# Fewer, longer transfers at the end of a graph attention layer: x of blocks 24 to 27 in one load, results of 8 to 23 stored by four blocks, 28 and 29 in one store

## The chip, the cores and the metric

The kernel runs on one core of a Trainium2 chip. The metric is the device time of one execution in microseconds (us). The kernel before took 235.53 us, the median of three runs (235.43, 235.53 and 236.7).

A core has five engines that work side by side, each with its own order of instructions: TensorE (PE; PEld is its weight load), VectorE (DVE), ScalarE (ACT), GpSimd (POOL) and SyncE (SP, which here only issues DMAs). Engines wait for each other, and for DMAs, on semaphores. 16 DMA engines move the data between the chip's memory (HBM) and the on-chip buffers; they serve SP's queue of ordinary transfers (q1 in the profile) and GpSimd's queue of gathers (q0).

## The reference

`x` has 4096 rows of 512, `adj` is 4096 by 4096, `W` is 512 by 4 x 512, `a` holds 2 x 512 weights for each of 4 heads.

```python
ht = (h @ W).reshape(N, N_HEADS, N_HIDDEN).transpose(1, 0, 2)
src = jnp.einsum('hnd,hd->hn', ht, a_src)
dst = jnp.einsum('hnd,hd->hn', ht, a_dst)
e = jax.nn.leaky_relu(src[:, :, None] + dst[:, None, :], SLOPE) + adj_mat[None]
att = jax.nn.softmax(e, axis=-1)
h_prime = jnp.einsum('hij,hjd->hid', att, ht)
x = _layernorm(x + h_prime.mean(axis=0), axis=-1)
```

`adj` is added to the scores, and its entries reach 1e9. So in a row the column with the largest entry of `adj` takes the whole softmax, wherever it leads by more than the scores can differ.

## The kernel before

**What it computes.** `leading_rows` takes the leading column of each row: the output row is the layer norm of x[i] + x[column] times the mean of W over the heads. A bound on the scores, from the norms of x and of the heads' vectors, tests whether each row's leader leads by enough; only where a row fails does `general` (the full softmax) run, which it doesn't with these inputs.

**Blocks.** The 4096 rows are 32 blocks of 128, NB = 32; partition p holds rows 32p to 32p + 31, one of each block. So neighbouring blocks of one partition lie side by side in HBM: a transfer of n blocks of x or of the output moves n x 2 KB in one piece for each partition. `hold` has all 32 blocks of x, is overwritten by the results, and in its upper half (blocks 16 to 31) first holds W. Q is 4, LATE is 28, BEHIND is 24.

**One step of the loop** (line 423, t from 0 to 31): load adj of block t + 5 (2 MB; blocks 28 to 30 in two pieces, 31 in four); take the maxima over segments of adj's rows (DVE, line 169); find the leading segment and fetch it again by a gather on GpSimd (`find_segment`, `fetch_segment`: row L185, gather L191); for block t - 2 find the column in the fetched segment (`find_column`: L214, L216) and gather the rows of x (`gather_rows`, L202); for t - 3 turn these rows (PE, L229), copy them (ACT, L231) and multiply them by the mean of W (L244); for t - 4 the moments; for t - 6 the normalising.

**Blocks 24 to 27.** Their x is loaded late, at t = 31 (line 440), two blocks at a time, after adj of block 31 in SP's order. Their products are put by in a freed buffer of adj (`put_by`), and x is added after the loop: `add_x`, L261, for 24, 25 and 26 on GpSimd, for 27 on VectorE. ACT takes their row norms with `row_norm` (L251).

**After the loop** (lines 479 to 542) the order is written out by hand, and each engine keeps it. GpSimd's is: add x to 24 (line 486), column and gather of 30 (487), fetch of the segment of 31 (488), add x to 25 (489), gather of 31 (490), add x to 26 (491). The column of 31 is searched in the whole row of adj (L222). VectorE takes `find_inner` of blocks 24 to 31 (L208) and then the test (`bound(3)`, L392, and `test`), which needs the fetched segment of 31. TensorE's order is: turn of 30, last product of 29, count of the test (L409), three products of 30, turn of 31, last product of 30, products of 31 in two halves (L286).

**The stores.** SP issues the stores of blocks 0 to 7 by four, of 8 to 23 by two, and then, when each is ready, 28, 29, 24 with 25, 26 with 27, 30 and 31 (lines 482 to 485 and 540 to 542). SP waits, before each DMA that it issues, until the DMA eight before it in its order has landed: eight semaphores go round.

Of the kernel before, what the change touches and what calls it, by code (L numbers as in the profile page):

```python
# [68 lines left out]
def leading_rows(ctx, tc, x, adj, W, a, out, ident, v, n_bad, any_bad):  # L69
# [8 lines left out]
    nc = tc.nc  # L78
    N, D = x.shape
    H = a.shape[0]  # L80
    KB, NB, S = D // P, N // P, N // E
    S_EARLY = N // E_EARLY
    AHEAD = 5
    Q = 4
    PIECES = 4
    LATE = NB - Q
    BEHIND = LATE - Q
# [29 lines left out]
    def load_adj(ib):  # L117
        if 0 <= ib < NB:
            t = adj_t[ib] = adj_pool.tile([P, N], F32, name="adj_t")
            n = pieces(ib)  # L120
            for k in range(n):
                nc.sync.dma_start(t[:, ts(k, N // n)], adj_rows[ib][:, ts(k, N // n)])

    def load_x(lo, n):
        nc.sync.dma_start(hold[:, ds(lo, n), :], x_rows[:, ds(lo, n), :])
# [36 lines left out]
    def segment_maxima(ib, lo, hi):  # L162

        e = E_EARLY if ib < EARLY else E
        if lo == 0:
            seg_of[ib] = small.tile([P, N // e], F32, name=f"seg{e}", bufs=2)
        n = max(pieces(ib), 2)
        for k in range(lo * n // PIECES, hi * n // PIECES):
            nc.vector.tensor_reduce(  # L169
                seg_of[ib][:, ts(k, N // e // n)],  # L170
                adj_t[ib][:, ts(k, N // n)].rearrange("p (s e) -> p s e", e=e), axis=AX.X, op=OP.max,
            )

    def find_segment(ib):
        seg = seg_of.pop(ib)
        nc.vector.max(out=top[:, ib, :], in_=seg)
        at = at_of[ib] = small.tile([P, 8], U32, name="at")
        nc.vector.max_index(at, top[:, ib, :], seg)  # L178
        if ib < NB - 1:
            fetch_segment(ib)  # L180
# [29 lines left out]
    def find_column(ib):  # L210
        if ib < BEHIND:
            find_inner(ib)
        within = small.tile([P, 8], U32, name="within")
        nc.vector.max_index(within, top[:, ib, :], lead_of[ib])  # L214
        col = small.tile([P, 1], U32, name="col")
        nc.gpsimd.tensor_tensor(col, at_of.pop(ib), within[:, 0:1], op=OP.add)  # L216
        gather_rows(ib, col)
# [7 lines left out]
    def turn(ib):  # L225
        y = y_t.pop(ib)
        tp = psum.tile([P, KB, P], F32, name="tp", bufs=2)
        for kb in range(KB):
            nc.tensor.transpose(tp[:, kb, :], y[:, ts(kb, P)], ident)  # L229
        yt = yt_of[ib] = rows.tile([P, KB, P], F32, name="yt")  # L230
        nc.scalar.copy(yt, tp)  # L231

    def residual(ib):
        start = ib not in o_ps
        if start:
            o_ps[ib] = psum.tile([P, D], F32, name="o")
        nc.tensor.matmul(o_ps[ib], ident, hold[:, ib, :], start=start, stop=False)  # L237

    def products(ib, lo=0, hi=KB):
        start = ib not in o_ps  # L240
        if start:
            o_ps[ib] = psum.tile([P, D], F32, name="o")
        for kb in range(lo, hi):
            nc.tensor.matmul(  # L244
                o_ps[ib], yt_of[ib][:, kb, :], w_sum[:, kb, :],
                start=(start and kb == 0), stop=(kb == KB - 1),
            )

    def row_norm(ib):
        sq = rows.tile([P, D], F32, name="sq")  # L250
        nc.scalar.activation(sq, hold[:, ib, :], AF.Square, accum_out=xx[:, ib : ib + 1])  # L251

    def put_by(ib):

        if ib == BEHIND:
            o_ps["by"] = adj_pool.tile([P, N // D, D], F32, name="adj_t")
        nc.scalar.copy(o_ps["by"][:, ib - BEHIND, :], o_ps.pop(ib))
# [12 lines left out]
    def rstd(i):  # L270
        nc.gpsimd.tensor_scalar(sd[:, i], sd[:, i], 1.0 / D, EPS, op0=OP.mult, op1=OP.add)
        nc.gpsimd.tensor_tensor(sd[:, i], sd[:, i], power[:, : i.stop - i.start], op=OP.pow)  # L272
        nc.gpsimd.tensor_mul(nm[:, i], nm[:, i], sd[:, i])
# [54 lines left out]
    def store(queue, lo, n):  # L328
        queue.dma_start(out_rows[:, ds(lo, n), :], hold[:, ds(lo, n), :])

    def mean_of_heads(kb):
        o = psum.tile([P, D], F32, name="o")
        for h in range(H):
            nc.tensor.matmul(o, ident, hold[:, w_at + kb * H + h, :], start=(h == 0), stop=(h == H - 1))  # L334
        nc.scalar.activation(w_sum[:, kb, :], o, AF.Copy, scale=1.0 / H)  # L335
# [5 lines left out]
    def turn_a():  # L341
        tp = psum.tile([P, KB, P], F32, name="tp", bufs=2)
        for k in range(KB):
            nc.tensor.transpose(tp[:, k, : 2 * H], a_rows[:, ts(k, P)], ident[: 2 * H, : 2 * H])
        nc.scalar.copy(at_d, tp[:, :, : 2 * H])

    def turn_w(kb, h):
        tp = psum.tile([P, KB, P], F32, name="tp", bufs=2)
        for k in range(KB):
            nc.tensor.transpose(tp[:, k, :], hold[:, w_at + kb * H + h, ts(k, P)], ident)  # L350
        wt = rows.tile([P, KB, P], F32, name="wt")
        nc.scalar.copy(wt, tp)  # L352
        return wt

    def head_vector(kb, h, wt):

        for k in range(KB):
            nc.tensor.matmul(  # L358
                pv[:, kb, h : 2 * H : H], wt[:, k, :], at_d[:, k, h : 2 * H : H],
                start=(k == 0), stop=(k == KB - 1),  # L360
            )

    def head_norms():
        nc.vector.tensor_copy(v, pv)
        vv = once.tile([P, KB, 2 * H], F32, name="vv")
        nc.vector.tensor_mul(vv, v, v)
        pn = psum.tile([P, KB, 2 * H], F32, name="px", bufs=1)
        nc.tensor.matmul(pn, ones, vv, start=True, stop=True)
        n2 = once.tile([P, 2 * H], F32, name="n2")
        nc.vector.tensor_reduce(n2, pn.rearrange("p k c -> p c k"), axis=AX.X, op=OP.add)  # L370
        nc.scalar.activation(n2, n2, AF.Sqrt)
        both = once.tile([P, H], F32, name="both")
        nc.vector.tensor_add(both, n2[:, :H], n2[:, H:])
        nc.vector.tensor_reduce(vn, both, axis=AX.X, op=OP.max)
# [48 lines left out]
    for t in range(NB):  # L423
        if t == NB // 2:
            tc.mark_branch_hint_location("general", engines=HINTED)
        if t in x_at:
            load_x(*x_at[t])
        if t + AHEAD == NB - 1:
            load_x(LATE, Q)
        load_adj(t + AHEAD)  # L430
        middle = 1 if t == NB - 1 else 2
        segment_maxima(t, 0, middle)
        if t >= COLUMN:
            find_column(t - COLUMN)
        segment_maxima(t, middle, PIECES)
        pair = FINISH <= t < BEHIND + FINISH and t % 2 == 0
        if pair:
            rstd(slice(t - FINISH, t - FINISH + 2))
        if t == NB - 1:
            for ib in (BEHIND, BEHIND + 2):  # L440
                load_x(ib, 2)
        find_segment(t)
        if t < 2:
            mean_of_heads(t)
        elif t == 2:
            mean_of_heads(2)
            mean_of_heads(3)
        if t == 0:
            turn_a()
        turned = [(*vectors[0], turn_w(*vectors.pop(0))) for _ in range(vectors_at.get(t, 0))]  # L450
        if t == 16:
            head_norms()
        ib = t - PROJECT
        if t == NB - 1:
            for late in range(LATE, NB):
                row_norm(late)
        if t == NB - 2:
            residual(LATE)
            residual(LATE + 1)
        if ib >= 0:  # L460
            turn(ib)
            if ib > BEHIND:
                products(ib - 1, KB - 1, KB)
            if ib < BEHIND:
                residual(ib)
        for some in turned:
            head_vector(*some)
        if ib >= 0:
            products(ib, 0, KB if ib < BEHIND else KB - 1)
        if t >= BEHIND + STATS:  # L470
            put_by(t - STATS)
        elif t >= STATS:
            stats(t - STATS)
            row_norm(t - STATS)
        if pair:
            finish(t - FINISH)
            finish(t - FINISH + 1)
# [1 line left out]
    for ib in range(BEHIND, LATE):  # L479
        row_norm(ib)  # L480
    nc.scalar.activation(xx, xx, AF.Sqrt)
    for ib in range(0, 2 * Q, Q):
        store(nc.sync, ib, Q)
    for ib in range(2 * Q, BEHIND, 2):
        store(nc.sync, ib, 2)
    add_x(nc.gpsimd, BEHIND)
    find_column(NB - 2)
    fetch_segment(NB - 1)
# [48 lines left out]
    moments(NB - 1)  # L537
    factor(NB - 1, shift=True)
    finish_in_halves(NB - 1)
    for ib, n in ((NB - 4, 1), (NB - 3, 1), (BEHIND, 2), (BEHIND + 2, 2), (NB - 2, 1)):  # L540
        store(nc.sync, ib, n)
    store(nc.sync, NB - 1, 1)

# [152 lines left out]
```

## Time and profile before

| | |
|---|---|
| median of three runs | 235.53 us |
| the profiled execution | 235.65 us |
| its span in the profile | 234.1 us |
| busy: PE, DVE, ACT, POOL | 197.5, 191.6, 111.6, 100.3 us |
| moved by DMA | 97.06 MB, 415 GB/s in the mean |
| x of 24 and 25: issued, from issue to landing | 193.05, 15.5 us |
| x of 26 and 27: issued | 195.79 |
| store of 0 to 3 issued, store of 31 issued | 199.23, 229.70 |
| gather of x for block 31: issued, from issue to landing | 215.40, 7.1 us |

Times inside an execution are us from the start of the span. A row of an engine's order of time gives the start, the busy time, the engine, the line, the operation, out<-in with shapes, how many were merged, and in brackets the idle time before and what ended it. In the chain of waits each row is the start, the time and what the end was waiting for then; "issue" is time in which nothing that the profile shows was waited for. A DMA row gives the number of transfers, the size of each and the median time from issue to landing. The digits of a slice are tenths of it busy, 9 for 90% or more.

### The profile page before, as it was taken

To read this page: it belongs to the slowest core of one execution; us is meant where nothing else is said; L and a number is where in the kernel's file an instruction comes from. 1 tells how busy PE (TensorE), PEld (TensorE's weight loads), DVE (VectorE), ACT (ScalarE), POOL (GpSimd) and SP (SyncE) were. 2 spreads that over 40 slices of the span, in tenths; PEclk is the share of its full clock that TensorE was granted. 3 is DMA by queue.
4 is the path that set the end of the run, shared out by engine and by line. 5 is a ranking of instruction groups with operands and counts; after the bars stand their busy time and mean duration, and the time that the engine had idled before them with its cause. 6 is when DMAs were issued, how large, how long until landed. Compare 5 with 4: busy or idle time off the path is not lost.

```text
span 234.1 us, 2486 instructions
## 1 busy us (share of the span) xinstructions
PE 197.5 (84%) x683; PEld 101.6 (43%) x683; DVE 191.6 (82%) x300; ACT 111.6 (48%) x267; POOL 100.3 (43%) x212
## 2 busy tenths in 40 slices
PE   0198959999999699999999599859899967999980
PEld 0034525765656356555544144324333423344360
DVE  0566885589929999999789986999999999989871
ACT  2003012155665447475768264645564654187561
POOL 2022232415524464646443642646465464557400
PEclk9999778999999999999999979999999999999997
DMA  6999999999999999999999999999999999999994
GB/s 243 432 428 417 445 419 434 418 444 420 433 422 427 430 424 433 426 419 431 434 427 427 429 433 424 419 436 419 435 428 417 425 427 421 413 426 419 416 386 179
DMA packets 12977, 97.06 MB, mean 415 GB/s; under 512 B 2072, under 2 KB 2584, under 8 KB 7200
## 3 DMA queue, kind: packets, MB, share of 16 engines
q1 hardware_dynamic: 9360, 88.08, 89.0%
q0 software_dynamic: 3584, 8.77, 9.5%
q8 instruction: 6, 0.10, 0.2%
q14 instruction: 11, 0.09, 0.1%
q10 hardware_dynamic: 16, 0.02, 0.0%
HBM read 88.47 MB, written 8.39 MB: 414 GB/s over the span
## 4 chain that ended last, share of the span: by engine, by line
DMA 48%; POOL 19%; issue 17%; DVE 11%; PE 2%; ACT 0%; POOLq 0%; DVEq 0%; ACTq 0%; SPq 0%
DMA adj_t<-in_adj_dram 41%; DVE seg L169 8%; POOL y L202 6%; POOL lead L191 5%; DMA y<-in_x_dram,col 3%; DMA lead<-in_adj_dram,row 2%; POOL sd L272 2%; PE o L286 2%; DMA a_rows<-in_L_gnn_a_dram 1%; DVE col L222 1%; POOL row L185 1%; POOL start L198 1%; POOL col L216 1%; POOL lead_early L191 1%; DVE at L178 1%
## 5 line engine op out<-in xcount | busy, mean ns | idle before, releaser
L169 DVE TENSOR_REDUCE seg<-adj_t 128x128 f32<-128x2048 f32 (+2 forms) x66 | 145.4, 2207 | 29.0 <-DMA adj_t<-in_adj_dram 29.0
L244 PE MATMUL o<-w_sum,yt 128*128 128x512 f32 x248 | 116.0, 609 | 0.7 <-ACT yt L231 0.7
L244 PEld LDWEIGHTS o<-w_sum,yt 128*128 128x128 f32 x248 | 44.8, 193 | 53.9 <-issue 42.4
L231 ACT COPY yt<-tp 128x512 f32<-128x512 f32 x32 | 18.8, 587 | 45.8 <-PE tp L229 45.7
L202 POOL DMA_INDIRECT y<-in_x_dram,col x32 | 30.8, 961 | 16.5 <-POOL col L216 15.4
L334 PE MATMUL o<-hold,ident 128*128 128x512 f32 x32 | 20.9, 815 | 14.6 <-DMA hold<-in_L_gnn_W_dram 14.6
L229 PE MATMUL tp<-ident,y 128*128 128x128 f32 x128 | 19.7, 276 | 13.7 <-DMA y<-in_x_dram,col 13.7
L237 PE MATMUL o<-hold,ident 128*128 128x512 f32 x52 | 26.8, 600 | 0.0
L229 PEld LDWEIGHTS tp<-ident,y 128*128 128x128 f32 x128 | 14.4, 141 | 26.8 <-issue 25.5
L185 POOL TENSOR_TENSOR row<-at,first 128x1 uint32<-128x1 uint32 x32 | 6.0, 188 | 43.7 <-DVE at L178 43.3
L352 ACT COPY wt<-tp 128x512 f32<-128x512 f32 x16 | 9.2, 586 | 31.5 <-PE tp L350 31.5
L191 POOL DMA_INDIRECT lead_early<-in_adj_dram,row x18 | 18.1, 1008 | 8.9 <-POOL row L185 8.9
L216 POOL TENSOR_TENSOR col<-start,within 128x1 uint32<-128x1 uint32 x31 | 5.8, 188 | 36.0 <-DVE within L214 36.0
L251 ACT ACTIVATE sq<-hold 128x512 f32<-128x512 f32 x32 | 19.8, 619 | 0.0
L358 PEld LDWEIGHTS pv<-at_d,wt 128*128 128x128 f32 x128 | 16.3, 191 | 6.8 <-ACT wt L352 3.7
L334 PEld LDWEIGHTS o<-hold,ident 128*128 128x128 f32 x32 | 8.1, 265 | 25.1 <-issue 20.2
L335 ACT ACTIVATE w_sum<-o 128x512 f32<-128x512 f32 x4 | 2.4, 598 | 33.0 <-PE o L334 33.0
L277 ACT ACTIVATE hold<-o,nm,sd 128x512 f32<-128x512 f32 x24 | 17.2, 769 | 0.0
L191 POOL DMA_INDIRECT lead<-in_adj_dram,row x14 | 14.0, 1003 | 7.0 <-POOL row L185 7.0
L268 ACT ACTIVATE sq<-o,nm 128x512 f32<-128x512 f32 x24 | 16.5, 687 | 0.8
L358 PE MATMUL pv<-at_d,wt 128*128 128x2 f32 x128 | 15.3, 244 | 0.6 <-ACT wt L352 0.6
L266 ACT ACTIVATE sq<-o 128x512 f32<-128x512 f32 x24 | 14.6, 609 | 0.0
(91 smaller groups left out, 150.8 us busy)
## 6 DMA issues: line engine op xcount, KB each, us to landing
adj_t<-in_adj_dram SPq DMA_DIRECT2D x28, 2048.0 KB, 31.7
adj_t<-in_adj_dram SPq DMA_DIRECT2D x6, 1024.0 KB, 28.0
out_dram<-hold SPq DMA_DIRECT2D x10, 512.0 KB, 14.3
hold<-in_L_gnn_W_dram SPq DMA_DIRECT2D x4, 1024.0 KB, 18.8
hold<-in_x_dram SPq DMA_DIRECT2D x2, 2048.0 KB, 36.5
hold<-in_x_dram SPq DMA_DIRECT2D x3, 1024.0 KB, 27.8
adj_t<-in_adj_dram SPq DMA_DIRECT2D x4, 512.0 KB, 19.7
out_dram<-hold SPq DMA_DIRECT2D x2, 1024.0 KB, 13.8
```

Source lines behind the costliest of these rows:

```text
L169: nc.vector.tensor_reduce(seg_of[ib][:, ts(k, N // e // n)], adj_t[ib][:, ts(k, N // n)].rearrange("p (s e) -> p s e", e=e), axis=AX.X, op ...
L191: nc.gpsimd.indirect_dma_start(out=lead, out_offset=None, in_=adj_segs_early if early else adj_segs, in_offset=bass.IndirectOffsetOnAxis(a ...
L202: nc.gpsimd.indirect_dma_start(out=y, out_offset=None, in_=x, in_offset=bass.IndirectOffsetOnAxis(ap=col[:, :1], axis=0),)
L229: nc.tensor.transpose(tp[:, kb, :], y[:, ts(kb, P)], ident)
L231: nc.scalar.copy(yt, tp)
L237: nc.tensor.matmul(o_ps[ib], ident, hold[:, ib, :], start=start, stop=False)
L244: nc.tensor.matmul(o_ps[ib], yt_of[ib][:, kb, :], w_sum[:, kb, :], start=(start and kb == 0), stop=(kb == KB - 1),)
L251: nc.scalar.activation(sq, hold[:, ib, :], AF.Square, accum_out=xx[:, ib : ib + 1])
L268: nc.scalar.activation(sq, o, AF.Square, bias=nm[:, i], accum_out=sd[:, i])
L277: nc.scalar.activation(hold[:, ib, :], o_ps.pop(ib), AF.Identity, bias=nm[:, i], scale=sd[:, i])
L334: nc.tensor.matmul(o, ident, hold[:, w_at + kb * H + h, :], start=(h == 0), stop=(h == H - 1))
L358: nc.tensor.matmul(pv[:, kb, h : 2 * H : H], wt[:, k, :], at_d[:, k, h : 2 * H : H], start=(k == 0), stop=(k == KB - 1),)
```

## The change

The two loads of x of blocks 24 and 25 and of 26 and 27 become one load of four blocks. The stores of blocks 8 to 23 go by four blocks (four stores of 1 MB) and not by two (eight of 512 KB). The stores of 28 and of 29 become one. In this stretch SP issues 11 stores and one load of x where it issued 16 stores and two loads.

```diff
@@ -437,8 +437,7 @@
         if t == NB - 1:
-            for ib in (BEHIND, BEHIND + 2):
-                load_x(ib, 2)
+            load_x(BEHIND, Q)
         find_segment(t)
@@ -479,10 +478,8 @@
     nc.scalar.activation(xx, xx, AF.Sqrt)
-    for ib in range(0, 2 * Q, Q):
+    for ib in range(0, BEHIND, Q):
         store(nc.sync, ib, Q)
-    for ib in range(2 * Q, BEHIND, 2):
-        store(nc.sync, ib, 2)
     add_x(nc.gpsimd, BEHIND)
@@ -537,7 +534,7 @@
     finish_in_halves(NB - 1)
-    for ib, n in ((NB - 4, 1), (NB - 3, 1), (BEHIND, 2), (BEHIND + 2, 2), (NB - 2, 1)):
+    for ib, n in ((LATE, 2), (BEHIND, 2), (BEHIND + 2, 2), (NB - 2, 1)):
         store(nc.sync, ib, n)
     store(nc.sync, NB - 1, 1)
```

The bytes, the arithmetic and the order of the transfers in SP's queue stay as they were, but that 28's result now goes with 29's.

## The prediction

> **What bounds the kernel now.** I read the page's slices first, then the chain of waits of the last 34 us, GpSimd's and TensorE's order of time there, and last the DMA packet records.
>
> The slices (40 of 5.85 us) and the DMA issues of the page:
>
> ```profile
> DMA  6999999999999999999999999999999999999994
> GB/s 243 432 428 417 445 419 434 418 444 420 433 422 427 430 424 433 426 419 431 434 427 427 429 433 424 419 436 419 435 428 417 425 427 421 413 426 419 416 386 179
> ...
> out_dram<-hold SPq DMA_DIRECT2D x10, 512.0 KB, 14.3
> ...
> hold<-in_x_dram SPq DMA_DIRECT2D x2, 512.0 KB, 15.5
> ```
>
> The DMA engines are full in every slice but the first and the last. The rate shows no drop where transfers shrink: 413 to 426 GB/s in the slices of the half-megabyte stores, 417 to 445 in those of the 2 MB loads. So only the last few us can be gained or lost by order. The chain there:
>
> ```profile
> 210.14 3.29 DVE col L222 x2
> 213.42 0.02 issue
> 213.44 1.28 POOL adj_t L261
> ...
> 215.40 7.09 DMA y<-in_x_dram,col
> 222.49 0.14 issue
> 222.62 0.63 PE tp L229 x4
> ```
>
> It ends with the gather of block 31's rows of x; the rest, turn, products, moments and normalising, takes 7.2 us from there to the last store, issued at 229.7. GpSimd's own order of time:
>
> ```profile
> 208.75 1.27 POOL L261 TENSOR_TENSOR adj_t<-adj_t,hold 128x512 f32<-128x512 f32 x1 [1.86 <-ACT sq L251]
> 210.22 0.19 POOL L216 TENSOR_TENSOR col<-start,within 128x1 uint32<-128x1 uint32 x1 [0.20 <-DVE within L214]
> 211.01 0.97 POOL L202 DMA_INDIRECT y<-in_x_dram,col  x1 [0.60 <-POOL col L216]
> 212.00 0.20 POOL L185 TENSOR_TENSOR row<-at,first 128x1 uint32<-128x1 uint32 x1
> 212.46 0.96 POOL L191 DMA_INDIRECT lead<-in_adj_dram,row  x1 [0.27 <-POOL row L185]
> 213.44 1.28 POOL L261 TENSOR_TENSOR adj_t<-adj_t,hold 128x512 f32<-128x512 f32 x1
> 215.40 0.96 POOL L202 DMA_INDIRECT y<-in_x_dram,col  x1 [0.67 <-issue]
> ```
>
> The first row is the sum that adds x of block 24. The page names ACT as its releaser, but that ACT work was over 0.6 us before; x of 24 landed at 208.54 (issued 193.05, 15.5 us), 0.21 us before it starts. From there GpSimd has 0.2 us of air up to the gather of block 31. Its last add ends at 214.72, VectorE's column of 31 at 210.21 + 4.42 = 214.63: the two arms that release that gather end 0.1 us apart.
>
> **The skill beside the trace.** "DMA: Bandwidth & Descriptors" (the Trainium skill), section "Rules for kernel authors", asks for transfers of at least 1 MiB, which would favour the change. This trace bears on it with the rates above, and with its packets: 0.160 us for one of 4 KB, 0.310 us for one of 8 KB, 0.085 us for one of 2 KB. Doubling a packet saves about 0.01 us of it, not a fixed cost of a transfer, as eight transfers are in flight. The same page, "Queues, rings and completion order", says that an engine alternates between its queues packet by packet. This trace agrees: gathers of y (4 packets of 4 KB an engine) land in 7.6 to 7.7 us while SP's packets are of 16 KB, in 6.6 to 6.7 while they are of 8 KB, and in 6.2 (block 30) while they are of 4 KB. I go by these rows: a gather beside 8 KB packets is about 0.5 us later than beside 4 KB ones.
>
> **The change, part by part**, all against the profiled execution: 235.65 us, of which 234.1 are the span and 1.55 lie around it.
>
> *Less packet time.* Stores of 8 to 23: 1024 packets of 4 KB become 512 of 8 KB, 1024 x 0.1597 - 512 x 0.3095 = 5.1 us of engine time; x of 24 to 27: 1.3; 28 and 29: 256 of 2 KB become 128 of 4 KB, 1.2. Together 7.6 us over 16 engines, 0.47 us. That shortens the queue, not the chain.
>
> *x of 24 to 27 in one.* SP waits for the landing of the transfer eight before, so the one transfer is issued at 193.05, as the first half was. It lands when all of it is there. The second half lands now at about 209.85 (the store that reuses its semaphore is issued at 209.91); 0.08 us fewer of packets make it 209.77. The first add on GpSimd then starts at 209.98 instead of 208.75. **Queued behind it**: column and gather of 30, segment row of 31 and its fetch, the add of 25, the gather of 31. With 0.2 us of air they all move by 1.23 - 0.20 = 1.03 us; the gather of 31 goes out at about 216.4. ScalarE's squares of 24 to 27 (from 209.63) move by 0.3 us and have 1.2 us of air before the turned copy at 213.67: nothing.
>
> *Stores of 8 to 23 by four.* Four transfers fall away here and one at the load, so each store waits for an earlier landing and goes out sooner (the last of them at about 205.5 instead of 215.5). SP's queue is first in, first out and full for 14 us: the bytes move in the same order, nothing gained. Their results were normalised by 195.5, so no store waits for data. But the gathers of 30 and 31 and the fetch of 31 now run beside 8 KB packets. The fetch of 31 is also queued behind the gather of 30, whose packets span 1.9 us beside 8 KB packets and 1.3 beside 4 KB: it lands 1.03 + about 0.5 = 1.5 us late, at 219.2 or so instead of 217.7.
>
> *28 and 29 together.* Block 28 now waits for 29, normalised at 222.1: its store goes out some 6 us later, about 223.6 with the rest of the delay. The queue holds the stores up to 23 until about 225 (now: 28 to 30 and 24 to 27 are 4.6 us of packets that end near 230, so 23 ends near 225.4): no gap opens before it. After it the queue has gaps of up to about 1 us, as 24 to 27 become ready late; below I use them.
>
> **Two arms meet at the turn of 31** (now 222.62).
> Arm one, the gather: issue 216.4 and 6.65 us gives 223.05. The present one took 7.09 because one of 16 engines finished 0.7 us after the others (landings at 221.75 and 222.49), where an instruction fetch of 8 KB fell among its packets. If that comes again, 223.9.
> Arm two, TensorE's order:
>
> ```profile
> 217.85 0.14 DVE L392 TENSOR_TENSOR lead_by<-px,vn 128x1 f32<-128x1 f32 x1
> ...
> 219.20 0.22 PE L409 MATMUL px<-gap,ones 128*1 128x32 f32 x2 [0.18 <-DVE gap L405]
> 219.35 2.84 PE L244 MATMUL o<-w_sum,yt 128*128 128x512 f32 x6
> 222.62 0.63 PE L229 MATMUL tp<-ident,y 128*128 128x128 f32 x4 [0.43 <-DMA y<-in_x_dram,col]
> ```
>
> The test needs the fetch of 31 (landed 217.71, so L392 follows at 217.85). The count and the products of 30 stand before the turn of 31, with 0.43 us of air. 1.5 us late, they end at 222.19 + 1.5 = 223.7.
> The later arm puts the turn at 223.3 to 224.1; I take 1.25 us late. The rest of the chain keeps its length: the last store is issued at 229.70 + 1.25 = 230.95.
>
> **The cover.** From the issue of the last store (now 229.70) to its first packet on a free engine is 0.84 us, its eight packets 0.7: done at 231.24 on fifteen engines. One engine still sends 4 KB packets of an earlier store until 230.9 and ends at 232.2; its completion is the one the end waits for. It lags since a 16 KB instruction fetch took it for 0.97 us at 225.9. After the change, the gaps between the late stores let such an engine catch up, so the last store ends on all engines at 230.95 + 1.55 = 232.5. The end moves by 232.5 - 232.2 = **0.3 us**: 235.65 + 0.3 = 235.95. The profiled execution stands 0.12 above the median, 235.53, so I write **235.9**.
>
> **Rivals.**
> 1. *The cover is gone* (slower). An instruction fetch or the longer backlog of 24 to 27 leaves one engine a full us behind at the end again, and the stray engine in the gather of 31 comes again as well: 1.25 to 1.5 us are paid in full, **237.0**. For it: fetches of 8 and 16 KB fall in this stretch now, and the delay moves them along with the work. Against it: the gaps of up to 1 us. It decides once the last store is issued later than about 231.8, or an engine's backlog passes that time.
> 2. *The queue is the bound* (not slower). If the add of x is not on the path, because x lands with its first half's time or GpSimd has more air than I read, only the 0.47 us of packets count: **235.1**. For it: the DMA is full to 229. Against it: most engines run empty between 230.3 and 230.5, before the last store's first packet.
> 3. *The transfers merge nothing on the chip*, as each is cut into rows of a partition anyway. Packets of 8 KB appear already where stores go by four, so this is not so.
>
> **Numbers.** My forecast 0.58, rival 1 0.27, rival 2 0.12, the rest something else. 0.5% or 1.2 us is what can be told from no change: 234.35 to 236.7. Rival 1 lies mostly above it, and a tenth of the forecast's spread too: slower 0.31. Rival 2 lies inside it for the most part: faster 0.06. Same 0.63. Range: down to rival 2, 235.0; up to rival 1 and a little more, 237.2.
>
> **What would show it.** The add of 24 starts near 210.0; the gather of 31 is issued near 216.4 and takes 6.6 to 7.6 us; L392 follows the fetch of 31 at about 219.3; the turn of 31 starts at 223.3 to 224.1; stores of 8 to 23 are all issued by 206; the last store is issued near 231.0 and lands within 2.3 us (now 3.1). I am wrong if the gather of 31 goes out where it did, or if the end follows some engine's backlog rather than the last store's own latency.

## The result, and the profile after

The changed kernel takes 236.1 us in the median of 15 runs (235.89 to 238.03), the kernel before 235.56 (15 runs, 235.38 to 236.7). The ratio is 1.0034, with a 95% interval of 1.002 to 1.0048: 0.5 us slower in the median, 0.8 by the ratio. The profiled execution took 235.96 us with a span of 234.3; before it was 235.65 and 234.1. The executions of most kernels fall into a cheaper and a dearer group, whose shares differ between kernels (of the changed one eight lie at 235.89 to 236.10 and seven at 236.49 to 238.03), so below the lowest time stands beside each median.

The slices and the DMA issues of the changed kernel's page:

```profile
DMA  6999999999999999999999999999999999999984
GB/s 234 437 425 420 445 418 434 417 438 424 436 423 426 429 427 429 427 427 422 434 429 435 422 430 427 417 439 417 435 425 418 427 425 422 415 424 428 422 348 191
...
out_dram<-hold SPq DMA_DIRECT2D x6, 1024.0 KB, 19.2
...
out_dram<-hold SPq DMA_DIRECT2D x3, 512.0 KB, 4.3
```

The rate while the stores run (slices 34 to 38: 422 to 428 but for one of 415) is hardly higher than before. The slice before the last fell from 386 to 348 GB/s: the same bytes are spread further towards the end. The 1 MB stores take longer from issue to landing because they are issued sooner and stand in the queue. What came late shows in GpSimd's order of time:

```profile
209.96 1.28 POOL L261 TENSOR_TENSOR adj_t<-adj_t,hold 128x512 f32<-128x512 f32 x1 [3.45 <-ACT yt L231]
211.19 0.19 POOL L216 TENSOR_TENSOR col<-start,within 128x1 uint32<-128x1 uint32 x1
211.66 0.97 POOL L202 DMA_INDIRECT y<-in_x_dram,col  x1 [0.27 <-POOL col L216]
212.64 0.20 POOL L185 TENSOR_TENSOR row<-at,first 128x1 uint32<-128x1 uint32 x1
213.11 0.96 POOL L191 DMA_INDIRECT lead<-in_adj_dram,row  x1 [0.27 <-POOL row L185]
214.09 1.28 POOL L261 TENSOR_TENSOR adj_t<-adj_t,hold 128x512 f32<-128x512 f32 x1
215.53 0.96 POOL L202 DMA_INDIRECT y<-in_x_dram,col  x1 [0.16 <-PE px L385]
```

The add of 24 starts at 209.96, 1.21 us later than before; the one load landed at 209.75. The gather of 30 and the fetch of 31 go out 0.65 us late, the gather of 31 only 0.13. The chain of waits now runs through the fetch of 31, no longer through the gather of 31:

```profile
213.11 6.30 DMA lead<-in_adj_dram,row
...
219.63 0.07 DVE lead_by L392
...
220.90 0.22 PE px L409 x2
221.12 2.77 PE o L244 x6
223.89 0.44 PE tp L229 x4
```

The fetch takes 6.30 us (before 5.25) and lands at 219.41, 1.70 late. The test, the count and the products of 30 follow it without a pause, and the turn of 31 starts at 223.73 where it started at 222.62.

### The profile page after: what moved, and what is told of

Its sections match the earlier page's. It is cut to its first block, busy times and chain, and to the rows that moved or that the text cites. A ratio compares the mean times of both kernels' runs of the same rounds, so it can differ in the third digit from the quotient of the medians.

```text
span 234.3 us, 2472 instructions
## 1 busy us (share of the span) xinstructions
PE 199.2 (85%) x683; PEld 103.2 (44%) x683; DVE 191.7 (82%) x300; ACT 111.6 (48%) x267; POOL 100.1 (43%) x212
## 4 chain that ended last, share of the span: by engine, by line
PE 28%; DMA 23%; issue 21%; POOL 21%; ACT 3%; DVE 2%; POOLq 0%; DVEq 0%
PE o L244 14%; DMA hold<-in_L_gnn_W_dram 11%; POOL y L202 6%; POOL lead L191 5%; DMA lead<-in_adj_dram,row 5%; DMA y<-in_x_dram,col 4%; PE pv L358 4%; DMA adj_t<-in_adj_dram 3%; PE o L237 3%; PE o L334 3%; POOL sd L272 2%; PE tp L229 2%; POOL lead_early L191 2%; PE tp L350 2%; PE o L286 2%
## 5 line engine op out<-in xcount | busy, mean ns | idle before, releaser
L334 PE MATMUL o<-hold,ident 128*128 128x512 f32 x32 | 21.9, 850 | 15.0 <-DMA hold<-in_L_gnn_W_dram 15.0
L237 PE MATMUL o<-hold,ident 128*128 128x512 f32 x52 | 27.7, 619 | 0.3 <-DMA hold<-in_x_dram 0.3
L229 PEld LDWEIGHTS tp<-ident,y 128*128 128x128 f32 x128 | 15.0, 143 | 24.8 <-issue 23.9
```

## The experiments

Three theories to begin with: *A*, the late load and the longer stores each delay the last gathers, and only together do they pass the air in TensorE's order and the cover at the end; *B* and *C*, the late load or the longer stores alone are the whole cost. The table has, from each profile, the times of the drain's chain. "F30" is when the fetch of 30's segment goes out, which measures how late the loop itself was; "F30 to turn" is from there to the turn of 31, so it compares drains alone. The landings are those of the DMA records. `reorder_b` and `kept_b` are the kernels `reorder` and `kept` profiled a second time: two profiles of one kernel differ by 0.22 and 0.46 us in "F30 to turn".

| kernel | F30 | gather of 30: issued, takes | fetch of 31 lands | F30 to turn of 31 | last store: issued, takes | median, lowest us |
|---|---|---|---|---|---|---|
| before | 204.23 | 211.01, 6.16 | 217.71 | 18.39 | 229.70, 3.14 | 235.56, 235.38 |
| the change | 203.97 | 211.66, 7.25 | 219.41 | 19.76 | 230.78, 2.39 | 236.1, 235.89 |
| x_one | 203.93 | 211.61, 6.65 | 218.82 | 19.21 | 230.19, 2.48 | 235.78, 235.4 |
| stores4 | 203.88 | 210.72, 6.98 | 218.19 | 18.81 | 229.77, 2.73 | 236.32, 235.05 |
| pair | 203.95 | 210.94, 6.28 | 217.66 | 18.58 | 229.61, 3.10 | 235.85, 235.44 |
| x_and_stores | 204.13 | 211.64, 7.28 | 219.42 | 19.61 | 230.79, 2.25 | 236.12, 235.65 |
| reorder | 205.06 | 211.79, 7.14 | 219.61 | 19.14 | 231.28, 2.41 | 236.0, 235.21 |
| reorder_b | 205.73 | 212.71, 7.33 | 220.51 | 19.36 | 232.17, 2.23 | 237.07, one execution |
| delay2 | 204.12 | 212.31, 6.25 | 218.99 | 19.19 | 230.36, 2.36 | 235.6, 235.29 |
| stores8 | 203.90 | 210.72, 8.62 | 221.20 | 21.61 | 232.56, 2.31 | 237.59, 236.91 |
| stores1 | 205.77 | 212.43, 6.08 | 219.03 | 18.00 | 230.82, 2.27 | 235.99, 235.71 |
| kept | 204.98 | 211.76, 6.52 | 218.95 | 19.14 | 231.20, 2.26 | 235.28, 234.98 |
| kept_b | 204.45 | 211.07, 6.59 | 218.35 | 18.68 | 230.21, 2.55 | 235.23, 235.06 |

**One part of the change at a time.** `x_one` has the load of four blocks alone, `stores4` the stores of 8 to 23 by four alone, `pair` 28 with 29 alone, `x_and_stores` the first two:

```diff
# x_one, x_and_stores
-            for ib in (BEHIND, BEHIND + 2):
-                load_x(ib, 2)
+            load_x(BEHIND, Q)
# stores4, x_and_stores
-    for ib in range(0, 2 * Q, Q):
+    for ib in range(0, BEHIND, Q):
         store(nc.sync, ib, Q)
-    for ib in range(2 * Q, BEHIND, 2):
-        store(nc.sync, ib, 2)
# pair
-    for ib, n in ((NB - 4, 1), (NB - 3, 1), (BEHIND, 2), ...
+    for ib, n in ((LATE, 2), (BEHIND, 2), ...
```

> Only x of 24 to 27 in one load. Theory A (two arms with 0.43 us of air, and an end covered by about 1 us by the slowest DMA engine; only load and stores together pass it): the add of 24 starts at 210.0, the gather of 30 goes out 0.65 us late (near 211.7), the fetch of 31 lands at 218.4 instead of 217.7, the turn of 31 starts near 222.9, and the end moves by -0.1 to +0.1 us. Rival B (the late x is the whole cost of the change): 0.4 to 0.6 us slower. Rival C (the stores are the whole cost): the fetch of 31 lands where it did.

Measured: ratio 1.0015 (1.0002 to 1.0027). The add of 24 starts at 209.91, the gather of 30 at 211.61. The fetch of 31 lands at 218.82, the turn of 31 starts at 223.14, a little later than theory A had it. C falls: the fetch moved although the stores are as before. The gather of 30 takes 0.49 us longer than in the kernel before, although 4 KB packets run beside it in both; theory A has no term for that. B isn't excluded by the time, whose interval, 0.05 to 0.6 us, holds B's range too; it falls with the next run.

> Only the stores of 8 to 23 by four. Theory A: GpSimd's order keeps its times; the gather of 30 takes 7.0 to 7.3 us instead of 6.2, the fetch of 31 6.0 to 6.3 instead of 5.2, so it lands near 218.7; the turn of 31 starts 0.5 to 0.7 us late, near 223.2, which the cover hides; 0.3 us fewer of packets: the time changes by -0.3 to +0.1 us. Rival B (the late x is the whole cost): 0.3 us faster, and the fetch of 31 lands where it did. Rival C (the stores are the whole cost): 0.4 to 0.6 us slower.

Measured: ratio 1.0016 (0.9997 to 1.0035), medians far apart, the lowest 0.3 us below. GpSimd's order keeps its pace, but the gather of 30 takes 6.98 us and the fetch of 31 6.01: it lands 0.48 late though the loop was 0.35 early. So B falls: the stores alone delay the fetch too. The time is unclear: six executions lie at 235.05 to 235.28, below the lowest of the kernel before (235.37), the other eight at 236.08 to 237.17. The profile is of one of the six, with a span of 233.5 against 234.1. Its turn of 31 comes 0.42 us later after F30, yet its last store lands 28.6 us after F30 as before: that delay is hidden. How much of the shorter span is the loop's early start, and how much the packets, the profile does not separate.

> Only 28 and 29 in one store. Theory A: the chain is untouched, the turn of 31 at 222.6; the store of 28 with 29 goes out at 222.1; 0.08 us fewer of packets: within 0.1 us of no change. Rival D (the late store of 28 leaves the queue empty and makes its end late): 0.3 to 0.7 us slower, with a gap in the DMA before 222 to 224.

Measured: ratio 1.0006 (0.9991 to 1.0021). The turn of 31 starts at 222.53, the last store at 229.61; the store of 28 with 29 goes out at 222.08. The DMA engines are full from 222 to 224 us (share 1.02, before 1.03), so the gap that D needs is not there; the time alone, -0.2 to 0.5 us, would not exclude D.

> The load in one and the stores by four, 28 and 29 apart. Theory A: the two delays add up on the fetch of 31, which lands 1.6 to 1.8 us late (near 219.4), the turn of 31 starts near 223.7, past the cover: 0.3 to 0.6 us slower, as the whole change. Rival D: no slower than before.

Measured: ratio 1.002 (1.0009 to 1.003), the fetch of 31 lands at 219.42, the turn of 31 starts at 223.74. These are the times of the whole change to 0.01 us, though its loop was 0.16 us later. In "F30 to turn" the load adds 0.82 us, the stores 0.42, both 1.22, the whole change 1.37: within the spread of two profiles the two add up. At the landing of the fetch, counted from F30, they add 1.41, 0.83 and together 1.81, less than the sum. The times of the runs are too close to split the 0.8 us the same way.

**Why the late load costs.** If it costs only because GpSimd's column, gathers and fetch are queued behind its add, moving that add behind them must give the time back. `reorder` is the whole change with

```diff
-    add_x(nc.gpsimd, BEHIND)
     find_column(NB - 2)
     fetch_segment(NB - 1)
-    add_x(nc.gpsimd, BEHIND + 1)
+    add_x(nc.gpsimd, BEHIND)
     find_column_in_row(NB - 1)
+    add_x(nc.gpsimd, BEHIND + 1)
     add_x(nc.gpsimd, BEHIND + 2)
...
-    stats(BEHIND + 1)
...
     turn(NB - 2)
+    stats(BEHIND + 1)
     stats(BEHIND + 2)
```

> The whole change, with GpSimd's add of x to 24 moved behind the fetch of 31's segment, the add to 25 behind the gather of 31, and ScalarE's sums of 25 behind the copy of 30. Theory A (the late x costs only because column, gathers and fetch are queued behind its add): gather of 30 near 210.9, fetch of 31 issued near 212.3 and landing near 218.3, turn of 31 near 222.7, last store near 229.8, and with 0.47 us fewer of packets a span of 233.3 to 233.7, 0.4 to 0.8 us below before. Rival B2 (the cost of the change lies in the packets beside the gathers alone): as the changed kernel, 234.1 to 234.4.

Measured: ratio 1.0021 (1.0004 to 1.0038); the lowest is 235.21. The span, 234.8, is not what A expected, but this execution came 0.83 us late into the drain. GpSimd's order of time in it:

```profile
211.00 0.19 POOL L216 TENSOR_TENSOR col<-start,within 128x1 uint32<-128x1 uint32 x1 [3.31 <-DVE within L214]
211.79 0.96 POOL L202 DMA_INDIRECT y<-in_x_dram,col  x1 [0.60 <-POOL col L216]
212.77 0.20 POOL L185 TENSOR_TENSOR row<-at,first 128x1 uint32<-128x1 uint32 x1
213.23 0.96 POOL L191 DMA_INDIRECT lead<-in_adj_dram,row  x1 [0.27 <-POOL row L185]
214.21 1.28 POOL L261 TENSOR_TENSOR adj_t<-adj_t,hold 128x512 f32<-128x512 f32 x1
```

The column waits for VectorE again, as before the change, and each row lies 0.77 to 0.78 us behind that of before, as the loop does (0.83): the late load no longer holds up GpSimd's order. F30 to turn is 19.14, 0.62 shorter than with the change. What is left, 0.75 us, comes with longer gathers: 7.14 us for that of 30, and 7.89 (before 7.09) for that of 31, which lands at 224.06, just ahead of the turn. So B2 is wrong on the mechanism: ten of the 22 executions, 235.21 to 235.43, lie below every one of the changed kernel. The median shows no gain over the kernel before.

> The reordered kernel once more, for a second profile: in the first the loop's work was already 0.8 us late when the fetch of 30 went out (205.06 instead of 204.23), by a longer stretch at half the clock near 82 us. With the fetch of 30 near 204 again, theory A expects the gather of 30 near 210.9, the fetch of 31 landing near 218.3, the turn of 31 near 222.9 and a span of 233.4 to 233.9.

Measured: one execution, 237.07 us, span 235.5. It didn't settle the span, as the loop was later still: the fetch of 30 went out at 205.73. F30 to turn is 19.36.

**Packets beside a gather.** `stores8` and `stores1` store 8 to 23 by eight blocks and by one:

```diff
-    for ib in range(2 * Q, BEHIND, 2):
-        store(nc.sync, ib, 2)
+    for ib in range(2 * Q, BEHIND, 2 * Q):   # stores8
+        store(nc.sync, ib, 2 * Q)
+    for ib in range(2 * Q, BEHIND):          # stores1
+        store(nc.sync, ib, 1)
```

> Stores of 8 to 23 by eight blocks, packets of 16 KB beside the last gathers; the rest as before. Theory A (a gather of y waits for one packet of SP's queue at each of its four): gather of 30 takes 8.0 to 8.6 us (before 6.2), fetch of 31 about 7.2 (before 5.2), the turn of 31 starts 1.0 to 1.8 us late: 0 to 0.8 us slower. Rival F (the longer gathers come from more stores standing in the queue, not from their packets): as with stores by four, 7.0 and 6.0 us.

> Stores of 8 to 23 one block at a time, packets of 2 KB; the rest as before. Theory A: gather of 30 takes 5.7 to 5.9 us, the chain is up to 0.3 us earlier, but the queue has 0.6 us more of packets and its slowest engine sets the end: 0.4 to 0.8 us slower. Rival E (the end follows the chain): 0 to 0.3 us faster.

Measured: `stores8` 1.0099 (1.0066 to 1.0132), `stores1` 1.0013 (1.0005 to 1.0021). The gather of 30 takes 6.08 us beside packets of 2 KB, 6.16 to 6.28 beside 4 KB, 6.98 beside 8 KB and 8.62 beside 16 KB where x of 24 to 27 comes in two loads. Where it comes in one, it takes 6.52 to 6.65 beside 4 KB and 7.14 to 7.33 beside 8 KB. In `stores4` and `stores8` all stores up to 23 stand in SP's queue when the gather goes out, the same bytes in six stores and in four, and the gather differs by 1.64 us: F falls. `stores8` cost more than expected, 2.0 us, because the fetch of 31 took 9.0 us, not 7.2. It stands behind the gather of 30 in GpSimd's queue, which was 2.5 us longer, and one DMA engine ended it at 221.20, the fifteen others by 220.38. `stores1` has the shortest chain of all (18.00), and is not faster. That speaks against E, but weakly: its profiled loop was 1.5 us late.

**The cover.** To delay the chain with no transfer changed, `delay2` and `delay4` put two and four idle adds on GpSimd:

```diff
     add_x(nc.gpsimd, BEHIND)
+    for k in range(2):                       # 4 in delay4
+        nc.gpsimd.tensor_add(o_ps["by"][:, Q + k, :], hold[:, 0, :], hold[:, 0, :])
```

> The kernel before, with two idle adds of 1.27 us each on GpSimd behind the add to 24; no transfer is changed. Theory A: gather of 30 and fetch of 31 go out about 1.9 us late, the turn of 31 starts 1.2 to 1.6 us late, and of that 0.7 to 1.0 us are hidden by the slowest DMA engine: 0.3 to 0.8 us slower. Rival E (nothing is hidden, the end follows the last store's issue): 1.2 to 1.6 us slower.

Measured: ratio 1.0003 (0.9989 to 1.0018). Its chain of waits:

```profile
213.76 5.23 DMA lead<-in_adj_dram,row
...
223.47 0.44 PE tp L229 x4
...
229.77 0.56 ACT hold L326
```

The turn of 31 is 0.69 us late, less than expected, the last store 0.66 late (230.36), and the span 234.0 against 234.1: all of it is hidden. The table says where: the last store takes 2.36 us instead of 3.14. In the kernel before, fifteen engines end that store by 231.86 and the last at 232.84; in `delay2` by 232.57 and at 232.72. In every kernel whose last store goes out after 230 this time is 2.2 to 2.55 us; where it goes out before, it is 2.7 to 3.1. The difference between 3.14 and 2.36, 0.8 us, is the cover. E falls.

> The kernel before, with four idle adds on GpSimd in place of two; no transfer is changed. With two, the turn of 31 started 0.7 us late and the end did not move. Two more are 2.55 us: the turn of 31 starts about 3.2 us late (near 225.8). Theory A (a cover of about 0.8 us at the end): the end moves by 2.2 to 2.6 us. Rival E (nothing is covered, the first 0.7 us were lost in the measurement): 3.0 to 3.3 us. Rival G (the queue can hide a delay of this size too): under 1.5 us.

Measured: ratio 1.0112 (1.008 to 1.0144), median 3.0 us slower, lowest 237.56, 2.1 above. G falls. The rest is unclear: the profiled execution (span 239.0) lost more at TensorE, whose clock was halved in the drain, so A and E can't be told apart here.

**What can be kept.** `kept` is `reorder` with the stores of 8 to 15, which stand beside the gather of 30 and the fetch of 31, by two again; `kept_b` is the same kernel once more.

```diff
-    for ib in range(0, BEHIND, Q):
+    for ib in range(0, 2 * Q, Q):
+        store(nc.sync, ib, Q)
+    for ib in range(2 * Q, 4 * Q, 2):
+        store(nc.sync, ib, 2)
+    for ib in range(4 * Q, BEHIND, Q):
         store(nc.sync, ib, Q)
```

> What the theory would keep of the change: x in one with the reordered adds, 28 and 29 together, stores of 16 to 23 by four, but 8 to 15, which are in flight beside the last gathers, by two. Theory A: gather of 30 about 6.2 us, fetch of 31 about 5.3 us as before, turn of 31 near 222.6, and 0.31 us fewer of packets: 0.1 to 0.4 us faster than before. Rival B2: no faster, or slower, as the x in one still costs.

> The kernel of the run kept once more, since its interval still holds no change: theory A expects 0.2 to 0.4 us faster in the median again, and a profile in which the fetch of 30 goes out near 204.2 as before, with gathers of about 6.2 us and a last store near 229.7.

Measured: `kept` 235.28 against 235.63, ratio 0.9992 (0.9975 to 1.0008); `kept_b` 235.23 against 235.6, ratio 0.9984 (0.9972 to 0.9997). The median is 0.35 us lower both times, and the second interval leaves no change just out. It is the best version tried, by about 0.15%. In the two profiles the gather of 30 takes 6.52 and 6.59 us and the fetch of 31 5.75 and 5.83, longer than I expected (6.2 and 5.3): beside 4 KB packets that is what `x_one` has too (6.65 and 5.75), so moving GpSimd's add does not take this part of the load's cost away. The gather of 31 still runs beside 8 KB packets (7.84 and 7.53 us, before 7.09), and the turn waits for it.

## Why the prediction was right

The forecast was 235.9 us; it is 236.1. The sum was made for the profiled execution, 235.95, which took 235.96; for the seven dearer executions it has no term. The mechanism is the one forecast: a late add and longer gathers delay the turn of 31, and the cover takes most of that. But two terms were off in opposite ways, 0.4 us too much and 0.6 too little, and that they nearly cancel is luck.

- *The add of 24 and what is queued behind it.* Predicted at 209.98, it starts at 209.96. "They all move by 1.03 us" was the mis-sized term: 0.65 for the gather of 30 and the fetch, 0.13 for the gather of 31. I took the pauses ahead of a gather for fixed. They fall from 0.60 to 0.27 and from 0.67 to 0.16 us when what the gather waits for has come before GpSimd gets there.
- *Gathers beside 8 KB packets.* "About 0.5 us later" was mis-sized the other way: 1.1 for the gather of 30 and 1.05 for the fetch. `stores4` shows 0.82 and 0.76 without the late load. The kernel before had that row: its gather of 29, issued at 205.93 beside stores with 8 KB packets, took 6.94 us; the 6.6 to 6.7 are gathers beside loads. The rest comes with the load in one, which lengthens the gather of 30 beside 4 KB packets as well (by 0.49 in `x_one`). Part of it passes before the gather's first packet: 4.17 to 4.35 us where x comes in two loads, 4.34 to 4.59 where it comes in one. Why stays open.
- *Two arms at the turn of 31.* The fetch was to land 1.5 us late and landed 1.70 late. TensorE's arm was to end at 223.7: its products end at 223.89, later by the fetch's 1.70, but the turn starts at 223.73 already, as the two overlap by 0.16 in the profile. The gather's arm was ready at 223.09 (223.05 predicted), by luck: it went out 0.9 us earlier than predicted and took 0.9 longer. The last store was to go out at 230.95 and went out at 230.78.
- *The cover.* The last store was to land within 2.3 us and took 2.39. Its landing moved by 0.33 us (232.84 to 233.17; 0.3 predicted), the span by 0.2. But its cause was wrong in one point. I put the slowest engine's lag down to the instruction fetch of 16 KB at 225.9. The landings show it earlier: the store of 12 and 13 ends on fifteen engines by 219.48 and on the last at 219.80, that of 14 and 15 by 221.34 and at 222.68. Between them falls the fetch of 8 KB at 220.2; that it is the cause was not tested. And the gaps did not let it catch up at once: in the changed kernel one engine still ends the store of 26 and 27 at 231.93, the others by 231.01. By the last store it has caught up (233.17, the others by 233.04).

The gaps themselves are there. The DMA share by stretches, before (the last two columns are the share and GB/s):

```profile
225.00:229.00 4.00, 2.64 (x13) 1.98 (x11) 2.92 (x12) 2.36 (x6) 0.00 (x0) 1.00 0.93 369
229.00:230.00 1.00, 0.00 (x0) 0.00 (x0) 0.53 (x2) 0.56 (x1) 0.00 (x0) 1.00 0.95 377
230.00:231.00 1.00, 0.00 (x0) 0.00 (x0) 0.00 (x0) 0.00 (x0) 0.00 (x0) 1.00 0.65 252
```

and in the changed kernel:

```profile
225.00:229.00 4.00, 3.72 (x17) 2.96 (x16) 3.28 (x11) 3.15 (x6) 0.00 (x0) 1.00 0.68 275
229.00:230.00 1.00, 0.00 (x0) 0.00 (x0) 0.57 (x4) 0.29 (x1) 0.00 (x0) 1.00 1.04 426
230.00:231.00 1.00, 0.00 (x0) 0.00 (x0) 0.61 (x2) 0.56 (x1) 0.00 (x0) 0.99 0.93 363
```

From 225 to 229 the engines now stand idle a third of the time, as 24 to 29 become ready late: the 0.47 us of packets that the change saves come back as idle time before the last results exist.

- *Rival 1* (237.0) has the time of the executions of 236.5 to 237.1, but no profile of the changed kernel was taken in one, so that they are dear by its mechanism is not shown. *Rival 2* (235.1) was wrong: the add of x is on the path. With the add moved, and 4 KB packets beside the gather of 30, a gain of its size shows in `kept` and `kept_b` (0.35 us).

## What to carry to other kernels

Where transfers are queued deep enough to keep the DMA engines full, longer ones save some 10 ns a packet, while all who wait for the first half of a merged load wait for its second, and so does everything queued behind them in their engine's order. Before merging, ask who waits for each half, and what gathers run beside the longer packets. And find out which of two ends is later, the queue's slowest engine or the last store's own time: a gain or a loss on the earlier one does not show.

## What the runs showed of the hardware

**A gather's time by the packets beside it** was the clearest row. With x in two loads the gather of 30 took 6.1, 6.2, 7.0 and 8.6 us beside stores with packets of 2, 4, 8 and 16 KB; with x in one load 6.5 to 6.65 beside 4 KB and 7.1 to 7.3 beside 8 KB. The packets do not set all of it: a gather of the kernel before, issued at 195.95, took 7.53 us beside packets that were nearly all of 4 KB. "DMA: Bandwidth & Descriptors" (the Trainium skill), section "Queues, rings and completion order", has an engine change queues only between packets, and a packet there is some 9 to 17 descriptors. How many descriptors a record of the trace is, the trace does not say, but its records fit a change after each one: on average the gather's four records of an engine start 0.29, 0.42 and 0.76 us apart beside records of 4, 8 and 16 KB, close to the 0.16 us of one of its own and the 0.16, 0.31 or 0.61 of one of theirs. Its closing record of 4 bytes starts one more such step later (0.27, 0.42 and 0.76). So four packets at 0.15 us more each, an estimate of 0.6 from 4 to 8 KB, fall short of the 0.82 measured in `stores4`: from the first packet to the closing record 0.56 is added, the rest before and after.

**A late start of the drain.** In eleven of the fourteen profiles TensorE's clock is halved for a stretch that begins at 79 to 83 us. The stretch from 78 to 92 us (after the length and the five engines' busy times come the granted clock, the DMA share and GB/s), before:

```profile
78.00:92.00 14.00, 12.20 (x53) 7.16 (x52) 13.59 (x20) 7.53 (x18) 7.16 (x14) 1.00 1.02 432
```

in `reorder`:

```profile
78.00:92.00 14.00, 10.97 (x37) 6.63 (x36) 13.59 (x19) 3.43 (x9) 7.26 (x15) 0.76 1.01 428
```

in `reorder_b`:

```profile
78.00:92.00 14.00, 10.11 (x27) 6.03 (x28) 13.59 (x19) 2.85 (x8) 7.33 (x15) 0.63 1.02 433
```

The fetch of 30 goes out at 203.88 to 204.23 in the eight profiles without such a stretch or with one of 3.4 us; at 203.93, 204.45, 204.98 and 205.06 with one of 6.8 us (`x_one`, `kept_b`, `kept`, `reorder`); at 205.73 and 205.77 with one of 10.2 us (`reorder_b`, `stores1`). So each late drain follows a long stretch more than 100 us earlier, but `x_one` has a long one and no late drain. That the stretch delays the drain is therefore likely, not shown: no run changed the clock alone. Once a late drain has used the cover, I infer, a longer chain is paid in full; that the changed kernel's dearer executions are of this kind was not profiled. "TensorE: Matmul & The Clock Gate" (the Trainium skill), section "What's actually happening", states a free-running window of some 3.4 us and calls its effect run-variable; the stretches here are 3.4 to 10.2 us long, in multiples of it.
